# Second spectral product of a convolution and Fourier-mixing kernel: the 64-channel part as two products at TensorE row places 0 and 64, one PSUM tile and one store per half

## Chip, cores, metric

The kernel runs on one core of a Trainium2 chip. A time is the device time of one execution in microseconds (us), from the device's own counter. The profile is one execution recorded by the hardware profiler: its span is the time from the first to the last instruction of the program on that core.

## What is computed

The input is 32 images of 56 x 56 places with 96 channels, in float32. Each image goes through two layers. The first is a layer norm, a product to 192 channels, a 3 x 3 convolution back to 96, SiLU, and the residual. The second takes the 3136 places as a sequence and runs a Fourier mixing step and a feed-forward step. The change lies in the Fourier mixing step, which in the reference reads:

```python
h = jnp.einsum('bnc,hc->bnh', x, w1)
h = jax.nn.relu(_bn(h, bn1_gamma, bn1_beta, bn1_mean, bn1_var))
X = jnp.fft.fft(h, axis=1, norm='ortho')
xr = jax.nn.relu(X.real * rd - X.imag * idg + rb)
xi = jax.nn.relu(X.imag * rd + X.real * idg + ib)
y = jnp.fft.ifft(xr + 1j * xi, axis=1, norm='ortho').real.astype(jnp.float32)
o = jnp.einsum('bnh,ch->bnc', y, w2)
return _bn(o, bn2_gamma, bn2_beta, bn2_mean, bn2_var)
```

There are 192 channels before the product with w2 and 96 after it. Because w2 acts on channels alone, the kernel applies it to the spectrum, ahead of the inverse transform.

## The kernel before

**Stages.** Each image passes through the steps of the class `Image`: layer norm and image layout (`im`), convolution in three groups of 32 output channels (`cv`, lines 182 and 186), back to places (`st`, line 219), second norm and turn to channels (`tp_n`, line 158), product with w1 (`ph`, line 232), the first half of the transform (`pa`, line 241), a trip through DRAM that regroups the places (`da`, `at`), the second half of the transform (`px`, line 256), scale and ReLU of the spectrum into `gt`, the product with w2 (`pg`, lines 295 and 299), the first half of the inverse (`pe`, line 309), a second trip through DRAM (`de`, written at line 501, read into `y` at line 507), the last part of the inverse (`py`, line 317), and the feed-forward step in fp8 (`tp_n` line 156, `pf` line 328, `po` line 342). Work of several images is in flight at a time.

**The stage that is changed.** The 28 pages of an image's spectrum are worked in four units of 8, 8, 8 and 4 pages (`UNITS`). A page is a matrix of 192 channels by 112 columns (114 in the first unit). Channels 0 to 127 of a page fill the 128 partitions of `gt[:, 0]` or `gt[:, 1]`. The last 64 channels of two pages share the partitions of `gt[:, 2]`: channels of a page of the unit's first half lie at partitions 0 to 63, those of the matching page of its second half at partitions 64 to 127. So one `gt[:, 2, j]` belongs to two pages.

`product_w2` (line 289) takes two such pairs at a time, chosen by `four` (line 284). For each pair it issues one product over 128 partitions with the weights `w2y`, which are 192 columns wide and zero in the off-diagonal blocks, so that one result holds both pages side by side (line 295). Then it adds, for each of the two pages, a product over 128 partitions with `w2x`, 96 columns wide (line 299). Both pairs lie in one PSUM tile `pg`. ScalarE copies it to `gw` (line 301), `inverse` multiplies each page by its table (line 309) into `pe`, ScalarE copies that to `es` (line 311), and `store_back` (line 496) issues two stores to `de`. Each image has 14 pairs: 14 products at line 295 and 28 at line 299.

**Records.** TensorE's stationary operand here is the page (112 or 114 columns) and the moving operand the weights. Each float32 matmul of these lines is two records of the trace (a weight load and a product each), so that 448 products of line 295 appear as 896. The text calls such a record a pass.

**What sets the order.** The kernel keeps a list `order` of steps with due times; `plan` (line 570) puts them there in units of an eighth of an image. `second_w2`, `second_back` and `store_back` of a unit are due at fixed distances (lines 653 to 657). The list's order is the priority with which the framework's scheduler lays out each engine's instructions when the kernel is built; a step whose inputs or buffers it expects late falls behind others. On the chip each engine then runs its list in that order. `pg`, `pe`, `pa` and `po` share the two PSUM buffers of the tag `b`.

**Tiles of the array.** The convolution puts four products of 32 columns side by side at column places 0, 32, 64 and 96 of the array, and `px` of the last 64 channels puts two of 64 columns at column places 0 and 64 (line 256, the form 112*64 in the trace; 112*128 is the whole array). All other products of a steady image address the array as a whole.

Of the kernel before, what the change touches and what calls it, by code (L numbers as in the profile page):

```python
# [38 lines left out]
F32 = mybir.dt.float32  # L39
# [6 lines left out]
C = 96  # L46
# [5 lines left out]
PG = 4  # L52
NS = NP // PG
UNITS = ((0, 8), (8, 16), (16, 24), (24, 28))
# [20 lines left out]
def width(p):  # L75

    return 2 * N2 + (p < UNITS[0][1])
# [8 lines left out]
def hybrid_kernel(ctx: ExitStack, tc: tile.TileContext, x, par, spar, cpar, w_in, conv_w, w1, w2, fw1, fb1, fw2, fb2, fa, fb, ib, ia, rows6, out):  # L86
    nc = tc.nc
    nb = x.shape[0]

    const = ctx.enter_context(tc.tile_pool(name="const", bufs=1))  # L90
# [12 lines left out]
    ib_sb = const.tile([114, NP, 112], F32, name="ib_sb")  # L103
# [6 lines left out]
    rows6_sb = const.tile([N1, 2 * WC * WG], F32, name="rows6_sb")  # L110
    w1a = const.tile([C + 1, H], F32, name="w1a")
    w2x = const.tile([128, C], F32, name="w2x")
    w2y = const.tile([128, 2, C], F32, name="w2y")
    w1q = const.tile([C, FF], F8, name="w1q")
    w2q = const.tile([128, 3, C], F8, name="w2q")
    b1q = const.tile([128, 3], F32, name="b1q")
# [164 lines left out]
        nc.vector.scalar_tensor_tensor(gt[:, u, :n, 0, :], sv[:, 0], rb, av[:, 1], ALU.add, ALU.max)  # L281
        nc.vector.scalar_tensor_tensor(gt[:, u, :n, 1, :], sv[:, 2], 0.0, sv[:, 1], ALU.max, ALU.subtract)  # L282

    def four(m, j0):

        p0, p1 = UNITS[m]
        return [[p0 + half * (p1 - p0) // 2 + j0 + j for j in range(2)] for half in range(2)]

    def product_w2(gt, b, m, j0):
        k = 2 * width(UNITS[m][0])  # L290
        pg = psum2.tile([k, 2, 2, C], F32, tag="b", name=f"pg_{b}_{m}_{j0}")
        for j in range(2):

            lhs = gt[:, 2, j0 + j].rearrange("c r k -> c (r k)")
            nc.tensor.matmul(pg[:, :, j, :], lhs, w2y, start=True, stop=False, skip_group_check=True)  # L295
            for half in range(2):
                p = four(m, j0)[half][j] - UNITS[m][0]
                lhs = gt[:, p // PG, p % PG].rearrange("c r k -> c (r k)")
                nc.tensor.matmul(pg[:, half, j, :], lhs, w2x, start=False, stop=True, skip_group_check=True)  # L299
        gw = work.tile([k, 2, 2, C], F32, tag="gw", name=f"gw_{b}_{m}_{j0}")  # L300
        nc.scalar.copy(gw.rearrange("k h j c -> k (h j c)"), pg.rearrange("k h j c -> k (h j c)"))
        return gw

    def inverse(gw, b, m, j0):

        pe = psum2.tile([112, 2, 2, C], F32, tag="b", name=f"pe_{b}_{m}_{j0}")
        for half, ps in enumerate(four(m, j0)):
            for j, p in enumerate(ps):
                nc.tensor.matmul(pe[:, half, j, :], ib_sb[: gw.shape[0], p, :], gw[:, half, j, :], start=True, stop=True)  # L309
        es = work.tile([112, 2, 2, C], F32, tag="es", name=f"es_{b}_{m}_{j0}")  # L310
        nc.scalar.copy(es.rearrange("k h j c -> k (h j c)"), pe.rearrange("k h j c -> k (h j c)"))
        return es

    def transform_out(y, b, g):
# [170 lines left out]
            im.gt[m] = work.tile([128, 3, PG, 2, w], F32, tag="gt", name=f"gt_{im.b}_{m}")  # L485
        relus(*im.held.pop(("sv", m, u)), im.gt[m], u)

    def second_w2(im, m, j0):
        im.gw[m, j0] = product_w2(im.gt[m], im.b, m, j0)

    def second_back(im, m, j0):
        if m + j0 == 0:
            im.de = dram.tile([NP, 112, C], F32, tag="de", name=f"de_{im.b}")
        im.held["es", m, j0] = inverse(im.gw.pop((m, j0)), im.b, m, j0)

    def store_back(im, m, j0):
        p0, p1 = UNITS[m]
        es = im.held.pop(("es", m, j0))
        rows = im.de[p0:p1].rearrange("(h j) m c -> m h j c", h=2)
        for half in range(2):  # L500
            nc.sync.dma_start(rows[:, half, j0 : j0 + 2], es[:, half])

    def fetch_y(im, g):
        if g < NG:
# [65 lines left out]
    def plan(b):  # L570
        im = Image(b)

        def put(when, f, *args):
            order.append((8 * b + when, len(order), lambda: f(im, *args)))

        last = b == nb - 1
        CONV, FIRST, BACK, FFN = ALL
        S0, SS = 0, 2
        if nb - 4 < b < nb - 1:
            BACK, FFN = BACK + 0.4, FFN + 0.284  # L580
        if last:

            CONV, FIRST, FFN = CONV - 0.074, FIRST - 0.016, FFN - 0.721
            S0, SS = -0.831, 2.033
        back_step, ffn_step = (0.82, 0.962) if last else (0.775, 0.971)

        for i, (j0, j1) in enumerate(LN_CHUNKS):
            at = CONV - 2.485 + 0.531 * i
            ahead = 12 if b == 0 else 2.489 - 0.157 * i
            put(CONV - 7.98 + 0.01 * i if b == 1 else at - ahead, fetch, i)  # L590
            put(at - 0.551, take_in, i)
            for j in range(0, j1 - j0, 2):
                put(at + 0.08 * j, make_image, i, j)
            put(CONV + (5.967 if b else 5.7) + 1.132 * i, norm_b, i)
            put(FIRST + 2 * i - (0.477 if b else 0.6), deviation, i)
            if b:
                put(CONV - 0.346 + 0.78 * i, load, i)
        put(CONV - 0.078, make_seam)
        for r in range(NR if b else 0):
            at = CONV + 1.91 * r  # L600
            for part, when in enumerate((0, 0.139, 1.039)):
                put(at + when, conv_part, r, part)
            put(at + 0.72, conv_first, r)
            put(at + 1.252, conv_last, r)
            for half in range(2):
                put(at + 1.757 + 0.21 * half, conv_tokens, r, half)
                put(at + 1.858 + 0.21 * half, conv_end, r, half)
        if b == 0:

            at = CONV  # L610
            for r in range(NR + 1):
                steps = []
                if r < NR:
                    steps += [(conv_part, r, 0), (conv_part, r, 1), (conv_part, r, 2), (conv_first, r)]
                if r:
                    steps += [(conv_tokens, r - 1, 0), (conv_end, r - 1, 0)]
                    steps += [(conv_tokens, r - 1, 1), (conv_end, r - 1, 1)]
                if r < NR:
                    steps += [(conv_last, r)]
                for f, *args in steps:  # L620
                    put(at, f, *args)
                    at += 0.214
        for g in range(NG):
            at = FIRST + g
            put(at - 0.407, tokens_a, g)
            for j2 in range(2):
                put(at + 0.065 + 0.371 * j2, forth, g, j2)
                put(at + 0.536 + 0.659 * j2, forth_a, g, j2)
            put(at + 1.2, store_a, g)
# [12 lines left out]
            put(at + 0.986, ffn_end, g)  # L642
            put(at + 1.497, store, g)
        for g in range(NS):
            put(max(FIRST + 7.433, S0 + g - (1.479 if g % 2 else 1.674)), fetch_a, g)
        for m, (p0, p1) in enumerate(UNITS):
            both = p1 - p0 > PG
            for at, u in ((0, 0), (0.606, 1), (1.099, 2)) if both else ((0.088, 0), (0.674, 2)):
                at += S0 + SS * m + (0.125 if m + u == 0 else 0)
                put(at, second, m, u)  # L650
                put(at + 0.22, second_parts, m, u)
                put(at + 0.47, second_relus, m, u)
            for j0 in range(0, (p1 - p0) // 2, 2):
                at = S0 + SS * m + (2.024 if both else 1.221) + 0.062 * j0
                put(at, second_w2, m, j0)
                put(at + 0.2, second_back, m, j0)
                put(at + 0.575, store_back, m, j0)

    def load(im, i):
        im.load(i)  # L660
# [3 lines left out]
    for b in range(nb):  # L664
        plan(b)
# [15 lines left out]
    with tc.tile_pool(name="setup", bufs=1) as sp, tc.tile_pool(  # L681
        name="setup_ps", bufs=2, space=bass.MemoryType.PSUM
# [16 lines left out]
        for g in range(2):  # L699
            ps = spp.tile([128, 512], F32, tag="ps", name=f"ps_wt{g}")  # L700
# [6 lines left out]
        for y in range(3):  # L707
            ps = spp.tile([128, 512], F32, tag="ps", name=f"ps_we{y}")
# [89 lines left out]
    def make_w2():  # L798
# [2 lines left out]
        scale, bias = bn_fold("2", BN2, 1)  # L801
        tc.keep_in_program_order(nc.vector.tensor_scalar(w2s[:, :H], w2s[:, :H], scale, None, ALU.mult))
        tc.keep_in_program_order(nc.vector.tensor_copy(w2s[:, H:], w2s[:, 128:H]))
        nc.gpsimd.memset(w2y, 0.0)
        ps = bank("w2")
        for g in range(2):
            nc.tensor.transpose(ps[:, g * C : (g + 1) * C], w2s[:, g * 128 : (g + 1) * 128], ident[:C, :C])
        tc.keep_in_program_order(nc.vector.tensor_copy(w2x, ps[:, :C]))
        for i in range(2):
            tc.keep_in_program_order(nc.vector.tensor_copy(w2y[64 * i : 64 * i + 64, i, :], ps[64 * i : 64 * i + 64, C : 2 * C]))  # L810
# [156 lines left out]
```

## Time and profile before

| quantity | value |
|---|---|
| median of three runs | 3042.79 us (3034.49 to 3044.51) |
| span of the profiled execution | 3036.8 us |
| TensorE (PE) busy | 2978.4 us, 98% |
| VectorE (DVE) busy | 2348.2 us, 77% |
| ScalarE (ACT) busy | 2277.4 us, 75% |
| line 295 (`pg` with `w2y`) | 896 passes, mean 335 ns |
| line 299 (`pg` with `w2x`) | 1792 passes, mean 258 ns |
| stores `de` (line 501) | 448, 84.0 KB each, 2.0 us to landing |

The page of the profile does not list a whole time of the profiled execution beside its span; the median of the runs is 6.0 us above the span (3042.79 - 3036.8), which is taken as what lies around it. A busy time of PE counts a product from its start to its modelled end, and successive products overlap, so mean durations cannot be added up. What a stretch costs is read from the timeline instead, as the distance between the start of its first row and the start of the row that follows it. The granted clock is 1.00 between 300 and 2800 us, so that durations of that stretch can be compared directly.

### The profile page before, as it was taken

How to read it: one execution, taken by the hardware profiler on the slowest of the kernel's cores; microseconds unless marked ns; L12 is line 12 of the kernel's file. 1: busy time of each engine (PE TensorE's matmuls, PEld its weight loads, DVE VectorE, ACT ScalarE, POOL GpSimd, SP SyncE). 2: the span in 40 equal slices, each digit the busy share in tenths (PEclk: the TensorE clock that was granted, in tenths of full speed). 3: DMA queues.
4: the chain of work that ended last, by engine and by line, in shares of the span. 5: the costliest groups of instructions: out<-in, count | busy, mean ns of one | idle time of the engine just before them, and what ended most of it. 6: DMA issues, size and time to landing. Idle time of an engine off the chain costs nothing.

```text
span 3036.8 us, 84414 instructions
## 1 busy us (share of the span) xinstructions
PE 2978.4 (98%) x32693; PEld 2445.3 (81%) x32693; DVE 2348.2 (77%) x7248; ACT 2277.4 (75%) x5703; POOL 647.5 (21%) x398
## 2 busy tenths in 40 slices
PE   8999999999999999999999999999999999999997
PEld 7678788888888887888888888888888888888775
DVE  5548777888778887778887778887778887777778
ACT  3467777787777787777787777787777877777877
POOL 2202122222112221122221222221222221121111
PEclk9899999999999999999999999999999999999998
DMA  3533444443454444444444444434444434444443
GB/s 85 144 93 94 117 126 124 118 123 98 121 133 126 117 116 108 122 130 122 123 109 114 125 126 123 127 98 122 124 128 122 123 96 124 129 129 104 113 123 78
DMA packets 495435, 355.37 MB, mean 117 GB/s; under 512 B 329992, under 2 KB 459304, under 8 KB 494808
## 3 DMA queue, kind: packets, MB, share of 16 engines
q1 hardware_dynamic: 493146, 349.24, 43.5%
q8 instruction: 257, 4.21, 0.6%
q10 hardware_dynamic: 1888, 0.74, 0.1%
q14 instruction: 144, 1.18, 0.1%
HBM read 195.73 MB, written 154.14 MB: 115 GB/s over the span
## 4 chain that ended last, share of the span: by engine, by line
PE 88%; DMA 5%; DVE 3%; ACT 2%; issue 1%; POOL 0%; SPq 0%; ACTq 0%; DVEq 0%
PE cv L186 14%; PE ph L232 10%; PE px L256 10%; PE pa L241 9%; PE im L165 7%; PE pe L309 6%; PE pg L299 5%; PE py L317 5%; PE pg L295 5%; PE po L342 4%; PE pf L328 4%; PE cv L182 3%; PE st L219 3%; PE tp_n L158 2%; DMA de<-es 2%; DMA xl<-in_x 1%
## 5 line engine op out<-in xcount | busy, mean ns | idle before, releaser
L186 PE MATMUL cv<-img,wv 97*32 97x196 f32 x13248 | 621.6, 331 | 0.0
L147 POOL TENSOR_TENSOR rs_c<-var_c,mhalf 112x8 f32<-112x8 f32 (+1 forms) x128 | 206.7, 1615 | 1894.1 <-DVE var_c L145 879.1
L186 PEld LDWEIGHTS cv<-img,wv 97*32 97x32 f32 x13248 | 426.8, 109 | 106.9
L235 ACT ACTIVATE h<-ph,rs_b 112x192 f32<-112x192 f32 x896 | 340.1, 449 | 74.1 <-PE ph L232 74.0
L232 PE MATMUL ph<-w1a,n2t 97*112 97x192 f32 x1792 | 381.2, 335 | 2.0 <-ACT n2t L225 0.9
L241 PE MATMUL pa<-h,fa_sb 112*112 112x384 f32 x896 | 372.3, 497 | 0.8 <-ACT h L235 0.8
L330 ACT CAST h<-pf 128x448 f16<-128x448 f32 x672 | 367.5, 567 | 1.1 <-PE pf L328 1.0
L256 PEld LDWEIGHTS px<-fb_sb,at 112*64 112x64 f32 (+1 forms) x3584 | 319.2, 166 | 58.1 <-issue 8.7
L256 PE MATMUL px<-fb_sb,at 112*64 112x112 f32 (+3 forms) x3584 | 353.5, 272 | 8.1 <-DMA at<-da 4.0
L165 PE MATMUL im<-rows_sb,xa 112*97 112x168 f32 x1792 | 321.2, 313 | 2.1 <-DVE xa L410 1.4
L232 PEld LDWEIGHTS ph<-w1a,n2t 97*112 97x112 f32 x1792 | 278.5, 177 | 47.4 <-issue 18.1
L147 POOL TENSOR_TENSOR rs_b<-var_b,mhalf 112x8 f32<-112x8 f32 (+1 forms) x128 | 227.7, 1788 | 397.3 <-DVE var_a L145 310.2
L165 PEld LDWEIGHTS im<-rows_sb,xa 112*97 112x97 f32 x1792 | 264.1, 168 | 33.1 <-issue 15.7
L242 ACT COPY u<-pa 112x384 f32<-112x384 f32 x448 | 226.2, 505 | 75.6 <-PE pa L241 75.4
L272 DVE SCALAR_TENSOR_TENSOR sv<-px,spar_sb,av 128x224 f32<-128x224 f32 (+2 forms) x352 | 152.9, 434 | 151.3 <-ACT av L263 149.8
L336 DVE CAST hq<-h 128x448 fp8e5<-128x448 f16 x672 | 256.1, 386 | 7.5
L335 DVE TENSOR_SCALAR h<-h,b1q 128x448 f16<-128x448 f16 x672 | 220.1, 329 | 40.6 <-ACT h L330 36.1
L299 PE MATMUL pg<-w2x,gt 128*112 128x96 f32 (+1 forms) x1792 | 243.1, 258 | 0.0
L167 ACT COPY img<-im 97x336 f32<-97x336 f32 x448 | 205.5, 461 | 48.6 <-PE im L165 25.8
L299 PEld LDWEIGHTS pg<-w2x,gt 128*112 128x112 f32 (+1 forms) x1792 | 240.8, 178 | 0.0
L261 ACT ACTIVATE av<-px,spar_sb 128x224 f32<-128x224 f32 (+2 forms) x352 | 162.8, 462 | 100.9 <-PE px L256 99.1
L295 PE MATMUL pg<-w2y,gt 128*112 128x192 f32 (+1 forms) x896 | 226.8, 335 | 1.1 <-DVE gt L282 0.7
(121 smaller groups left out, 6197.6 us busy)
## 6 DMA issues: line engine op xcount, KB each, us to landing
da<-u SPq DMA_DIRECT2D x224, 336.0 KB, 3.1
at<-da SPq DMA_DIRECT2D x224, 336.0 KB, 4.2
de<-es SPq DMA_DIRECT2D x448, 84.0 KB, 2.0
y<-de SPq DMA_DIRECT2D x224, 168.0 KB, 2.5
out<-t SPq DMA_DIRECT2D x224, 168.0 KB, 2.6
t<-in_x SPq DMA_DIRECT2D x96, 336.0 KB, 4.4
xl<-in_x SPq DMA_DIRECT2D x93, 336.0 KB, 4.5
t<-in_x SPq DMA_DIRECT2D x32, 168.0 KB, 3.8
```

The costliest lines, as they stand in the source:

```text
L147: nc.gpsimd.tensor_tensor(rs, var, mhalf[:, :n], ALU.pow)
L165: nc.tensor.matmul(ps[:, j], xa[:, j, :], rows6_sb, start=True, stop=True)
L186: tc.keep_in_program_order(nc.tensor.matmul(*args, start=(dx == 0), stop=(dx == 2)))
L232: nc.tensor.matmul(ph[:, j, :], n2t[:, 2 * j2 + j, :], w1a, start=True, stop=True)
L235: nc.scalar.activation(h[:, j], ph[:, j], AF.Relu, scale=rs[:, 2 * j2 + j : 2 * j2 + j + 1])
L241: nc.tensor.matmul(pa, fa_sb, h, start=True, stop=True)
L242: nc.scalar.copy(u[:, 2 * j2 : 2 * j2 + 2, :], pa)
L256: nc.tensor.matmul(px[rows, j], lhs, fb_sb[:, first(p) : first(p + 1)], start=True, stop=True)
L295: nc.tensor.matmul(pg[:, :, j, :], lhs, w2y, start=True, stop=False, skip_group_check=True)
L299: nc.tensor.matmul(pg[:, half, j, :], lhs, w2x, start=False, stop=True, skip_group_check=True)
L330: nc.scalar.copy(h1, pf)
L336: nc.vector.tensor_copy(hq[:, k, :], h2, saturate=False)
```

## The change

`w2y` loses its zero blocks: it is 96 columns wide, with the same 64 rows of weights once at partitions 0 to 63 and once at 64 to 127. A unit's product is made in two calls, one per half of its pages. The first call allocates a PSUM tile for each half and issues, for every pair, two products over 64 partitions each: partitions 0 to 63 (row place 0) into the tile of half 0, partitions 64 to 127 (row place 64) into the tile of half 1. These 8 products (4 in the last unit) stand together; all but the first are marked to be placed with high priority, in program order. The products with `w2x` of half 0 follow, then in the second call those of half 1. Copies, inverse and store go by halves: one copy to `gw`, one PSUM tile `pe`, one copy to `es` and one store for each. The due times of the two calls lie 0.124 apart, as those of the two blocks of a unit of 8 pages did.

```diff
-    w2y = const.tile([128, 2, C], F32, name="w2y")
+    w2y = const.tile([128, C], F32, name="w2y")
...
-        for j in range(2):
-
-            lhs = gt[:, 2, j0 + j].rearrange("c r k -> c (r k)")
-            nc.tensor.matmul(pg[:, :, j, :], lhs, w2y, start=True, stop=False, skip_group_check=True)
-            for half in range(2):
-                p = four(m, j0)[half][j] - UNITS[m][0]
-                lhs = gt[:, p // PG, p % PG].rearrange("c r k -> c (r k)")
-                nc.tensor.matmul(pg[:, half, j, :], lhs, w2x, start=False, stop=True, skip_group_check=True)
...
+    def product_w2(pg, gt, b, m, half):
+
+        k, n = 2 * width(UNITS[m][0]), pages(m)
+        products = []
+        if half == 0:
+            pg += [psum2.tile([k, n, C], F32, tag="b", name=f"pg_{b}_{m}_{i}") for i in range(2)]
+            for j in range(n):
+                for i in range(2):
+                    rows = slice(64 * i, 64 * i + 64)
+                    lhs = gt[rows, 2, j].rearrange("c r k -> c (r k)")
+                    products.append((pg[i][:, j], lhs, w2y[rows], j == 0, False))
+        for j in range(n):
+            p = half * n + j
+            lhs = gt[:, p // PG, p % PG].rearrange("c r k -> c (r k)")
+            products.append((pg[half][:, j], lhs, w2x, False, j == n - 1))
+        for at, (to, lhs, rhs, start, stop) in enumerate(products):
+            args = dict(start=start, stop=stop, skip_group_check=True)
+            if half or at in (0, 2 * n):
+                nc.tensor.matmul(to, lhs, rhs, **args)
+                continue
+            with tc.high_priority():
+                tc.keep_in_program_order(nc.tensor.matmul(to, lhs, rhs, **args))
+        gw = work.tile([k, n, C], F32, tag="gw", name=f"gw_{b}_{m}_{half}")
+        nc.scalar.copy(gw, pg[half])
         return gw
...
+    def store_back(im, m, half):
+        p0 = UNITS[m][0] + half * pages(m)
+        rows = im.de[p0 : p0 + pages(m)].rearrange("j m c -> m j c")
+        nc.sync.dma_start(rows, im.held.pop(("es", m, half)))
...
-            for j0 in range(0, (p1 - p0) // 2, 2):
-                at = S0 + SS * m + (2.024 if both else 1.221) + 0.062 * j0
-                put(at, second_w2, m, j0)
-                put(at + 0.2, second_back, m, j0)
-                put(at + 0.575, store_back, m, j0)
+            for half in range(2):
+                at = S0 + SS * m + (2.024 if both else 1.221) + 0.124 * half
+                put(at, second_w2, m, half)
+                put(at + 0.2, second_back, m, half)
+                put(at + 0.575, store_back, m, half)
```

In the setup the zeroing of `w2y` is dropped and its two copies write 96 columns each. `inverse` has the same products as before, sorted by halves.

More of the change, by code (lines that the diff above doesn't have):

```diff
@@ L282, in relus @@
         nc.vector.scalar_tensor_tensor(gt[:, u, :n, 1, :], sv[:, 2], 0.0, sv[:, 1], ALU.max, ALU.subtract)
[L284 to L291, printed above, removed]
-        for j in range(2):
-            lhs = gt[:, 2, j0 + j].rearrange("c r k -> c (r k)")
-            nc.tensor.matmul(pg[:, :, j, :], lhs, w2y, start=True, stop=False, skip_group_check=True)
-            for half in range(2):
-                p = four(m, j0)[half][j] - UNITS[m][0]
-                lhs = gt[:, p // PG, p % PG].rearrange("c r k -> c (r k)")
-                nc.tensor.matmul(pg[:, half, j, :], lhs, w2x, start=False, stop=True, skip_group_check=True)
-        gw = work.tile([k, 2, 2, C], F32, tag="gw", name=f"gw_{b}_{m}_{j0}")
-        nc.scalar.copy(gw.rearrange("k h j c -> k (h j c)"), pg.rearrange("k h j c -> k (h j c)"))
-        return gw
@@ L304, in inverse, with pages @@
[L304 to L311, printed above, removed]
+    def pages(m):
+        return (UNITS[m][1] - UNITS[m][0]) // 2
@@ L312, in inverse @@
+    def inverse(gw, b, m, half):
+        n = pages(m)
+        pe = psum2.tile([112, n, C], F32, tag="b", name=f"pe_{b}_{m}_{half}")
+        for j in range(n):
+            at = ib_sb[: gw.shape[0], UNITS[m][0] + half * n + j, :]
+            nc.tensor.matmul(pe[:, j, :], at, gw[:, j, :], start=True, stop=True)
+        es = work.tile([112, n, C], F32, tag="es", name=f"es_{b}_{m}_{half}")
+        nc.scalar.copy(es, pe)
         return es
@@ L486, in second_relus, with second_w2, second_back @@
         relus(*im.held.pop(("sv", m, u)), im.gt[m], u)
[L488 to L492, printed above, removed]
-            im.de = dram.tile([NP, 112, C], F32, tag="de", name=f"de_{im.b}")
[L494 to L501, printed above, removed]
+    def second_w2(im, m, half):
+        if half == 0:
+            im.held["pg", m] = []
+        im.gw[m, half] = product_w2(im.held["pg", m], im.gt[m], im.b, m, half)
+    def second_back(im, m, half):
+        if m + half == 0:
+            im.de = dram.tile([NP, 112, C], F32, tag="de", name=f"de_{im.b}")
+        im.held["es", m, half] = inverse(im.gw.pop((m, half)), im.b, m, half)
+    def store_back(im, m, half):
+        p0 = UNITS[m][0] + half * pages(m)
+        rows = im.de[p0 : p0 + pages(m)].rearrange("j m c -> m j c")
+        nc.sync.dma_start(rows, im.held.pop(("es", m, half)))
     def fetch_y(im, g):
@@ L803, in make_w2 @@
         tc.keep_in_program_order(nc.vector.tensor_copy(w2s[:, H:], w2s[:, 128:H]))
-        nc.gpsimd.memset(w2y, 0.0)
         ps = bank("w2")
@@ L809, in make_w2 @@
         for i in range(2):
-            tc.keep_in_program_order(nc.vector.tensor_copy(w2y[64 * i : 64 * i + 64, i, :], ps[64 * i : 64 * i + 64, C : 2 * C]))
+            tc.keep_in_program_order(nc.vector.tensor_copy(w2y[64 * i : 64 * i + 64, :], ps[64 * i : 64 * i + 64, C : 2 * C]))
         ps = bank("o2")
```

## Prediction

> **What bounds the kernel now.** I read the engine rows of the page first, then the same busy times for the steady stretch, then the timeline of TensorE at three places, then the groups by shape.
>
> ```profile
> PE 2978.4 (98%) x32693; PEld 2445.3 (81%) x32693; DVE 2348.2 (77%) x7248; ACT 2277.4 (75%) x5703; POOL 647.5 (21%) x398
> ...
> PE py L317 <- DMA y<-de: 10.1, 11, 3.4
> ...
> 300.00:2800.00 2500.00, 2492.87 (x27790) 2056.53 (x27789) 1979.06 (x6099) 1924.37 (x4831) 552.78 (x325) 1.00 0.45 120
> ```
>
> The first line is the page's, the second is PE's longest wait in total, the third the steady window (PE, weight loads, DVE, ACT, POOL busy; clock; DMA share). PE idles 7.1 of 2500 us there, at the full clock, while DVE (1979) and ACT (1924) have over 500 us free. So PE's own list of work is the time, and an edit counts by the PE time that it adds or removes. All waits for the second DRAM trip are 10.1 us.
>
> The second look is one unit of the changed stage, all 8 pages in a row:
>
> ```profile
> 1484.90 0.54 PE L295 MATMUL pg<-w2y,gt 128*112 128x192 f32 x2
> 1485.28 0.54 PE L299 MATMUL pg<-w2x,gt 128*112 128x96 f32 x4
> 1485.65 0.50 PE L295 MATMUL pg<-w2y,gt 128*112 128x192 f32 x2
> 1485.99 0.54 PE L299 MATMUL pg<-w2x,gt 128*112 128x96 f32 x4
> 1486.37 0.50 PE L295 MATMUL pg<-w2y,gt 128*112 128x192 f32 x2
> 1486.71 0.54 PE L299 MATMUL pg<-w2x,gt 128*112 128x96 f32 x4
> 1487.09 0.51 PE L295 MATMUL pg<-w2y,gt 128*112 128x192 f32 x2
> 1487.43 0.54 PE L299 MATMUL pg<-w2x,gt 128*112 128x96 f32 x4
> 1487.81 0.35 PE L328 MATMUL pf<-n3t,w1q 96*128 96x448 fp8e5 x1
> ```
>
> From start to start, the four wide products take 0.38 + 0.34 + 0.34 + 0.34 = 1.40 us and the eight narrow ones 0.37 + 0.38 + 0.38 + 0.38 = 1.51 us. A pass of 192 columns thus costs 0.175 us, one of 96 columns 0.094 us. The narrow pass is no cheaper although its moving side is halved, since each also loads a page of 112 columns: the eight passes of `pe`, again 112 loaded and 96 moving, run from 1399.88 to the next row at 1400.65, 0.096 us each. I take 0.096 us as the floor that a 112-column load sets.
>
> The third look is what TensorE does when it changes between the whole array and column places:
>
> ```profile
> 1405.38 0.81 PE L232 MATMUL ph<-w1a,n2t 97*112 97x192 f32 x4
> 1406.03 0.35 PE L328 MATMUL pf<-n3t,w1q 96*128 96x448 fp8e5 x1
> ...
> 1522.85 0.90 PE L232 MATMUL ph<-w1a,n2t 97*112 97x192 f32 x4
> 1523.69 1.00 PE L256 MATMUL px<-fb_sb,at 112*64 112x114 f32 x16
> 1524.62 0.35 PE L182 MATMUL cv<-img,wv 97*32 97x196 f32 x1
> ...
> 1526.75 0.91 PE L232 MATMUL ph<-w1a,n2t 97*112 97x192 f32 x4
> 1527.50 0.81 PE L241 MATMUL pa<-h,fa_sb 112*112 112x384 f32 x2
> ```
>
> The same four passes of `ph` take 0.65 us between whole-array neighbours, 0.75 us right after a convolution (1526.75 to 1527.50), and 0.84 us after one and ahead of the `px` that uses column places (1522.85 to 1523.69). So being first after a change costs 0.10 us (nothing of the weights was loaded ahead) and being last before one costs 0.09 us (the next load starts only when the product is out). A visit to another arrangement and back has two of each: 0.38 us.
>
> ```profile
> L256 PE MATMUL px<-fb_sb,at 112*128 112x112 f32 x1280 | 169.4, 276 | 1.5 <-DVE t L516 1.5
> L256 PE MATMUL px<-fb_sb,at 112*64 112x112 f32 x1280 | 82.5, 267 | 0.0
> ```
>
> Equal numbers of passes, busy 169.4 us with the whole array and 82.5 us at two column places: there, two products run at once. In the timeline the 16 passes take 0.93 us with 0.09 of change in them, 0.05 each.
>
> **The change part by part.** The order of TensorE's instructions in the built kernel says how the new products stand. In 64 units all 8 stand together; in 31 the first one is placed earlier, alone, and 7 follow; of the short units 28 have 4 together and 4 have 1 and 3; the first image has 8 alone. That is 170 visits to the row places.
>
> Removed: 448 wide products, 1.40 / 4 = 0.35 us each: 156.8 us.
>
> Added: 896 products over 64 partitions, 1792 passes. The trace has no product at row places. Bounds: two at once, each pair of passes at the load floor, 0.096 us, as the column places do; or one after the other, 0.096 us per pass. I take pairs, since the nearest row (112*64) pairs fully. A run of 8, 7, 4, 3 or 1 products takes 8, 8, 4, 4 or 2 such slots: 64 x 8 + 31 x (8 + 2) + 28 x 4 + 4 x (4 + 2) + 8 x 2 = 974 slots, 93.5 us. One after the other: 1792 x 0.096 = 172.0 us.
>
> Added: 170 visits. Bounds: nothing, if a change of row place is none for the array, and 0.38 us each, 64.6 us. I take 0.38, the price of every change of arrangement that the trace shows.
>
> The narrow products stay 1792 passes, now without a wide one before them that loads ahead: 1792 x 0.096 = 172.0 us against 448 x 1.51 / 4 = 169.1 us, +2.9 us.
>
> Moved with them: the built order changes between whole array and places 1077 times against 668 before; 340 are the 170 visits, which leaves 69 more by `cv` and `px`. One such visit is 0.09 and 0.10 on the way out and 0.09 and about a quarter of 0.10 on the way in for 32 columns, 0.31 us: 69 / 2 x 0.31 = 10.7 us.
>
> Hidden: ACT gets 64 more copies (the short unit's, halved), 0 to 0.48 us each (the median of `gw`); I take 0, as ACT has 23% free, and without that cover it would be up to 31 us. SP issues 192 fewer stores at 0.45 us, 86 us off its queue; behind them stand the fetches of `y`. The last store of an image is now due 0.124 of an eighth of 91.7 us later, 1.4 us, but between the last `pe` and the first `py` the built order has 9.6 or 11.2 us of PE work by turns where it had 9.9. PE's wait for `y` was 10.1 us in all: at best -10, at worst 0.3 us x 32 = +10; I take 0. Setup loses one memset, nothing.
>
> The wait that is added: both PSUM buffers of tag `b` must be free for the row-place products, since these write both halves. Queued behind a waiting product are all of PE's next items, and `pa`, `po` and `pe` use the same buffers. Bounds: 0, or one ACT copy of 0.48 us for each of 128 units, 61 us. PE's waits for `gw` were 0.7 us in all, so I take 0.
>
> Sum: -156.8 + 93.5 + 64.6 + 2.9 + 10.7 = +14.9 us, made against the span of 3036.8 us; the runs' median lies 6.0 us above it, and carries over: 3042.8 + 14.9 = 3058 us.
>
> **Two rules from the skill.** The Trainium skill, TensorEngine Tiling (Array Packing), Key Properties, says that going to another tiling mode, not merely another tile, drains TensorE; it gives no time, and the 0.09 us above agrees, for column places. The Trainium skill, TensorE: Matmul & The Clock Gate, Measured speedup vs the span model, reports 3.07 times for four row tiles; an estimate from that, 1.53 for two, would make 1792 / 1.53 = 1171 slots, 112.4 us, and the sum +33.8 us, 3077 us. No run here shows it yet.
>
> **Rivals.** *Free row places* (the other side): the array need not empty between whole rows and row places, because the columns stay 112 wide. Then the 64.6 us go: -49.7 us, 2993 us. It wins from a visit under 0.38 - 14.9 / 170 = 0.29 us. For it: all changes seen are of columns. Against: each of them costs the same 0.09 us, whatever the widths.
>
> *No pairs*: the loads of two row places follow each other, and the load sets the pace. +78.5 us more, 3136 us. For it: 112 columns of weights are as many as the whole array loads, where the paired rows load 64. Against: in the 112*64 row neither loads nor products follow one another.
>
> *Buffer waits*: half of the 61 us, 3088 us. For it: the first product stands alone in 35 units, so the scheduler expected the second buffer late there. Against: the 0.7 us.
>
> **How the numbers follow.** Forecast 0.50 (3058, its own range 3040 to 3080); free row places 0.22 (2993); no pairs 0.15 (3136); buffer waits 0.13 (3088). The range 2990 to 3110 leaves out no pairs and little else. A measurement can tell 0.3%, 9.1 us: faster is below 3033.7, slower above 3051.9. Faster: 0.22 and 0.02 of the forecast's spread. Same: 0.15 of the forecast. Slower: the remaining 0.33 of it, 0.15 and 0.13.
>
> **What would show it.** Right: products over 64 rows start in pairs some 10 ns apart, pairs 0.096 us apart; the pass before and the first after them are longer by 0.09 and 0.10 us; PE stays above 99% busy in the steady stretch. Wrong: passes of 64 rows 0.09 us apart one by one (no pairs); no longer neighbours (free row places); idle PE ahead of the new lines put down to ACT `gw`, `u`, `y` or `es` (buffer waits). The forecast falls if several small terms, each from two or three rows, lean one way, as +14.9 is small beside 156.8.

## The result, and the profile after

The changed kernel takes 3068.17 us (median of 4 runs, 3067.48 to 3071.0) against 3042.36 us before (4 runs, 3034.49 to 3044.51): a ratio of 1.0086, 95% interval 1.0071 to 1.0101, so 25.8 us slower. Its profiled run took 3067.48 us with a span of 3065.7 us, 28.9 us over the span before. The 1.8 us between its time and its span is what lies around a span; the runs of the kernel before that were measured later show the same 1.8. The 6.0 us given ahead of the prediction are thus 4 us too many: the profiled execution before was about that much faster than the median, which is why the spans differ by more than the medians.

The engine row of its page, and its steady stretch (PE, weight loads, DVE, ACT, POOL busy; granted clock; DMA share; GB/s):

```profile
PE 3004.8 (98%) x33589; PEld 2397.3 (78%) x33589; DVE 2345.1 (76%) x7248; ACT 2281.7 (74%) x5767; POOL 632.7 (21%) x397
```

```profile
300.00:2800.00 2500.00, 2492.48 (x28250) 1992.69 (x28249) 1961.82 (x6059) 1912.33 (x4850) 535.14 (x324) 1.00 0.46 118
```

PE is as busy as before (2492.48 of 2500 us, before 2492.87), at the same clock. So by the page the loss is longer PE work and not longer gaps (short waits that it doesn't show come below): PE's busy time rose by 26.4 us. PE's wait for the second DRAM trip (total us, times, longest):

```profile
PE py L327 <- DMA y<-de: 7.7, 10, 2.5
```

The wait for `y` fell from 10.1 to 7.7 us; the only longer one in total, of `st` for ScalarE, is 7.9 us where it was 7.2. Waits for ScalarE's copy `gw` are still 0.7 us. Next the timeline of PE at a unit whose row-place products stand together:

```profile
1492.39 0.81 PE L232 MATMUL ph<-w1a,n2t 97*112 97x192 f32 x4
1493.13 0.33 PE L305 MATMUL pg<-w2y,gt 64*112 64x96 f32 x1
1493.14 0.33 PE L308 MATMUL pg<-w2y,gt 64*112 64x96 f32 x1
1493.30 0.26 PE L305 MATMUL pg<-w2y,gt 64*112 64x96 f32 x1
1493.31 0.85 PE L308 MATMUL pg<-w2y,gt 64*112 64x96 f32 x13
1494.09 0.43 PE L305 MATMUL pg<-w2x,gt 128*112 128x96 f32 x2
1494.36 0.75 PE L308 MATMUL pg<-w2x,gt 128*112 128x96 f32 x6
1494.95 0.95 PE L305 MATMUL pg<-w2x,gt 128*112 128x96 f32 x8
1495.74 0.74 PE L165 MATMUL im<-rows_sb,xa 112*97 112x168 f32 x4
```

A unit's first product stands at L305, the ones marked with high priority at L308. So the first two rows of `w2y` are its first products at row place 0 and at row place 64: they start 0.01 us apart, a pair runs at once. The 16 row-place passes take 1493.13 to 1494.09, 0.96 us; the 16 narrow ones 1.65 us; and the `ph` ahead lasts 0.74 us instead of 0.65: in the trace the first weight load of the row places starts only at 1493.13, with their first product, so nothing is loaded ahead across the change of form (from whole array to row or column places, or back). Together 0.96 + 1.65 + 0.09 = 2.70 us, where the unit took 1.40 + 1.51 = 2.91 us before: 0.21 us gained. And a unit whose first product was placed earlier:

```profile
1471.67 0.81 PE L241 MATMUL pa<-h,fa_sb 112*112 112x384 f32 x2
1472.41 0.43 PE L305 MATMUL pg<-w2y,gt 64*112 64x96 f32 x2
1472.77 1.15 PE L256 MATMUL px<-fb_sb,at 112*128 112x112 f32 x8
1473.75 0.35 PE L338 MATMUL pf<-n3t,w1q 96*128 96x448 fp8e5 x1
1473.94 0.81 PE L232 MATMUL ph<-w1a,n2t 97*112 97x192 f32 x4
1474.60 0.35 PE L338 MATMUL pf<-n3t,w1q 96*128 96x448 fp8e5 x1
1474.88 1.02 PE L308 MATMUL pg<-w2y,gt 64*112 64x96 f32 x14
1475.83 0.43 PE L305 MATMUL pg<-w2x,gt 128*112 128x96 f32 x2
1476.10 0.75 PE L308 MATMUL pg<-w2x,gt 128*112 128x96 f32 x6
1476.69 0.95 PE L305 MATMUL pg<-w2x,gt 128*112 128x96 f32 x8
1477.48 0.35 PE L338 MATMUL pf<-n3t,w1q 96*128 96x448 fp8e5 x1
1477.67 1.04 PE L256 MATMUL px<-fb_sb,at 112*128 112x112 f32 x8
```

Two passes at place 0 alone take 0.36 us, the other 14 take 0.95, the narrow ones 1.65. To these come the neighbours: `pa` 0.74 instead of 0.65 us, the first `px` group 0.98 where the second one takes 0.88, `pf` 0.28 where another takes 0.19. In sum 3.24 us, 0.33 more than before. So whole runs gain and split ones lose more: a split adds one visit and two slots that nothing shares.

**Prices.** From start to start over 300 to 2700 us, the pass before a change of form costs 92 ns extra (`ph` ahead of the row places 255 ns, ahead of `pf` 162 ns) and the first pass after it 75 ns (the first narrow pass after a row-place run 174 ns, the others 99 ns). A change is 0.167 us, a visit 0.334 us. The first number holds for every form (91 to 94 ns ahead of row places and of both kinds of column places); the second depends on the pass that comes first (75 ns for `pg` and `pe`, 88 to 92 for `px`, `ph` and `pa`), so 0.167 us for changes other than those of the row places is an approximation. A pair of row-place passes takes 0.099 us, as a narrow pass does. By these prices a short unit with its 4 products in one piece takes 4 x 0.099 + 0.334 + 8 x 0.099 = 1.52 us, against 2 x 0.35 + 1.51 / 2 = 1.46 before: it loses, though nothing splits it.

### The profile page after: what moved, and what is told of

It reads as the page before. It is cut to its first block, busy times and chain, and to the rows that moved or that the text cites. A ratio compares the mean times of both kernels' runs of the same rounds, so it can differ in the third digit from the quotient of the medians.

```text
span 3065.7 us, 86119 instructions
## 1 busy us (share of the span) xinstructions
PE 3004.8 (98%) x33589; PEld 2397.3 (78%) x33589; DVE 2345.1 (76%) x7248; ACT 2281.7 (74%) x5767; POOL 632.7 (21%) x397
## 4 chain that ended last, share of the span: by engine, by line
PE 73%; DVE 12%; ACT 6%; DMA 6%; issue 2%; POOL 1%; SPq 0%; POOLq 0%; ACTq 0%; DVEq 0%
PE cv L186 13%; PE ph L232 8%; PE px L256 8%; PE pa L241 7%; PE im L165 6%; PE pg L305 5%; PE py L327 4%; PE pe L319 4%; PE pg L308 4%; PE cv L182 3%; PE po L352 3%; PE pf L338 3%; PE st L219 2%; PE tp_n L158 2%; DMA de<-es 2%
## 5 line engine op out<-in xcount | busy, mean ns | idle before, releaser
L186 PE MATMUL cv<-img,wv 97*32 97x196 f32 x13248 | 633.0, 331 | 0.0
L340 ACT CAST h<-pf 128x448 f16<-128x448 f32 x672 | 358.0, 556 | 28.4 <-PE pf L338 28.1
L256 PE MATMUL px<-fb_sb,at 112*64 112x112 f32 (+3 forms) x3584 | 360.2, 273 | 7.6 <-DMA at<-da 4.2
L241 PE MATMUL pa<-h,fa_sb 112*112 112x384 f32 x896 | 364.0, 493 | 1.0 <-ACT h L235 1.0
L338 PE MATMUL pf<-n3t,w1q 96*128 96x448 fp8e5 x672 | 223.0, 357 | 4.0 <-ACT h L340 2.6
L319 PEld LDWEIGHTS pe<-gw,ib_sb 112*112 112x112 f32 (+1 forms) x1792 | 202.5, 178 | 24.9 <-issue 5.3
L147 POOL TENSOR_TENSOR rs_a<-var_a,mhalf 112x8 f32<-112x8 f32 (+1 forms) x128 | 210.5, 1660 | 51.2 <-DVE var_a L145 51.2
```

Source lines behind the costliest of these rows:

```text
L147: nc.gpsimd.tensor_tensor(rs, var, mhalf[:, :n], ALU.pow)
L186: tc.keep_in_program_order(nc.tensor.matmul(*args, start=(dx == 0), stop=(dx == 2)))
L241: nc.tensor.matmul(pa, fa_sb, h, start=True, stop=True)
L256: nc.tensor.matmul(px[rows, j], lhs, fb_sb[:, first(p) : first(p + 1)], start=True, stop=True)
L319: nc.tensor.matmul(pe[:, j, :], at, gw[:, j, :], start=True, stop=True)
L338: nc.tensor.matmul(pf, w1q[:, k * 128 : (k + 1) * 128], n3t, start=True, stop=True)
```

## Experiments

A run gives its median, and its ratio to the kernel before measured beside it. All twelve kernels do the whole work of the reference. Due times are in eighths of an image, so that 0.1 is 1.1 us (0.1 x 91.8 / 8); the expectations of runs 9, 10 and 12 call them us.

**1. The halved structure without row places.** The weights `w2y` get their zero blocks back, and every row-place product becomes one over all 128 partitions, in the place where it stands.

```diff
-                    rows = slice(64 * i, 64 * i + 64)
-                    lhs = gt[rows, 2, j].rearrange("c r k -> c (r k)")
-                    products.append((pg[i][:, j], lhs, w2y[rows], j == 0, False))
+                    lhs = gt[:, 2, j].rearrange("c r k -> c (r k)")
+                    products.append((pg[i][:, j], lhs, w2y[:, i], j == 0, False))
```

> The changed kernel's halves, PSUM tiles, order and stores, but without row places: each 64-channel product runs over all 128 partitions with zeros in the other page's rows. Theory (a loaded page of 112 columns sets 0.096 us per pass, a visit to places costs 0.38 us): 1792 passes at 0.096 us are 172.0 us where the wide products took 156.8 (+15.2), the other narrow passes +2.9, no visits to row places, and the built order has 751 changes between whole array and column places where it had 668 (83 / 2 x 0.31 = +12.9): 3042 + 31 = 3073 us. So row places as placed in the changed kernel would be worth only about 5 us (3073 - 3068). Rival (the loss of the changed kernel is in the visits and the rest of the change costs nothing): 3060 us or less.

Measured: 3092.72 us, ratio 1.0177 (1.0155 to 1.0198). That is 20 us above the expectation, which gave the row places only 5 us. So the halves with 96-column products cost 53 us by themselves, the changes and waits of their order included, and the row places win some 25 us of it back, visits included (24.5 us between the two medians, 27.6 between the two losses). That they do nothing but harm is wrong; they can't pay for the narrow products.

**2. Runs in one piece.** For half 0 the narrow products go first and the row-place products follow as one run; the last of them ends half 0.

```diff
-                for i in range(2):
+                for i in (1, 0):
...
+        if half == 0:
+            products = products[2 * n :] + products[: 2 * n]
+            products = [(to, lhs, rhs, at == 0 or (at == n), at >= n) for at, (to, lhs, rhs, _, _) in enumerate(products)]
...
-            if half or at in (0, 2 * n):
+            if half or at in (0, n):
```

> The products over 128 partitions of half 0 come first, then all row-place products, the first of them into the second half's tile, so that they start only when both PSUM buffers are there and no unit's run is split (128 visits instead of 170, 896 slots instead of 974). Theory (the loss is in the visits and the split runs): 896 x 0.096 + 128 x 0.38 + 2.9 + (723 - 668) / 2 x 0.31 - 156.8 = -10.8, 3031 us; down to 3010 if all images take the 90.7 us that those without split runs take in the changed kernel. Rival (the halves themselves cost: two PSUM buffers held at once, later stores): no gain over the changed kernel, 3060 us or more, with PE idle ahead of the new lines.

Measured: 3218.9 us, ratio 1.0588 (1.0566 to 1.0609). The expectation missed by 188 us. The products themselves did what they should (start to start the row-place passes take 110.5 us, 125.8 in the changed kernel), but PE now waits. By tile:

```profile
PE py L330 <- DMA y<-de: 78.2, 28, 5.0
PE py L330 <- ACT h L235: 18.6, 26, 0.7
```

One of these waits in PE's timeline, and the windows around it (length; PE, weight loads, DVE, ACT, POOL busy; granted clock; DMA share; GB/s):

```profile
1491.03 1.62 PE L330 MATMUL py<-y,ia_sb 113*112 113x384 f32 x2 [4.42 <-DMA y<-de]
```

```profile
1488.00:1491.00 3.00, 0.00 (x0) 0.00 (x0) 0.21 (x1) 0.00 (x0) 0.00 (x0) 0.71 0.45 133
1491.00:1494.00 3.00, 2.97 (x10) 2.34 (x10) 1.31 (x4) 0.00 (x0) 0.00 (x0) 0.50 0.61 176
1494.00:1498.00 4.00, 4.00 (x50) 2.19 (x49) 1.66 (x5) 1.71 (x4) 0.00 (x0) 0.50 0.08 28
1498.00:1502.00 4.00, 4.00 (x21) 3.38 (x14) 1.65 (x4) 1.47 (x4) 0.00 (x0) 0.50 0.01 4
```

PE stands for 4.42 us, and then has the granted clock 0.50 for at least 11 us, though it is busy for nearly all of them. Half of 11 us is lost again, so the idle time is charged about twice. The clock records of the trace show it for the whole run: between 300 and 2800 us PE waits 22 times for 2.1 to 4.4 us, 64 us in sum; after 20 of these waits the clock is at 0.50 for 3.4 to 13.7 us, 174 us in sum. PE is busy for 166 of them, so that 83 us are lost again.

The wait has two sides. Between the last `pe` of an image and its first `py` stand 9.3 us of PE work in the trace, where the kernel before has 10.3 (images 7 to 26, the wait itself left out). And the data come later: from that last `pe` to the image's last store of `de` pass 4.0 us, from the store to the fetch of `y` 5.7 us, before 3.5 and 4.4. In the instance shown, SP starts the store at 1481.79 us, it lands at 1488.46, and SP issues the fetch at 1488.51, when PE has been waiting for almost two. So of the rival, later stores have a part in it; PE does not idle ahead of the new lines.

**3. Runs in one piece, the pairs apart.** As 2, with all products at row place 64 ahead of those at 0.

```diff
-            for j in range(n):
-                for i in (1, 0):
+            for i in (1, 0):
+                for j in range(n):
```

> As together, but all row-place products of half 1 stand before all of half 0, so that neighbours share a row place. Theory (two row places run at once only where neighbours alternate): the 896 slots become nearly 1792, +86 us on together at most, 3100 to 3117 us. Rival (each row place works off its own list, whatever the order): as together, 3031 us.

Measured: 3197.61 us, ratio 1.0515 (1.0484 to 1.0546). In time this says little, as its waits differ from those of run 2. By start to start, the row-place passes take 155.8 us, 45.3 more than in run 2, so running in pairs is worth at least that much. A run of 16 passes in its timeline:

```profile
1433.50 0.43 PE L308 MATMUL pg<-w2y,gt 64*112 64x96 f32 x2
1433.78 1.22 PE L311 MATMUL pg<-w2y,gt 64*112 64x96 f32 x14
1434.93 0.34 PE L308 MATMUL pg<-w2x,gt 128*112 128x96 f32 x1
```

1.43 us, where the same run in pairs takes 0.96 and 16 passes one by one would take 16 x 0.099 + 0.167 = 1.75. So the second place still overlaps the first in part: in the trace it starts 0.47 us after it, when four passes have run alone.

**4. Runs in two pieces.** As 2, with half of the narrow products, half of the run, then the rest: one more visit for each of 128 units, and no slot that a pair doesn't share.

```diff
+            narrow, paired, h = products[:n], products[n:], n // 2
+            products = narrow[:h] + paired[: 2 * h] + narrow[h:] + paired[2 * h :]
```

> As together, but each unit's run of row-place products is cut in two with whole-array products between: the same 896 slots, 256 visits instead of 128, and 671 instead of 723 changes by column places. Theory (a visit costs 0.38 us): together + 48.6 - 8.1, 3072 us. Rival (row places cost little to enter, and the loss of the changed kernel came with the split runs' buffers): within 10 us of together.

Measured: 3067.03 us, ratio 1.0084 (1.0066 to 1.0103), near the 3072 that were expected, and 152 us under run 2, although it does more. Its wait of `py` for `y` is 9.7 us. The built order has changed with the edit, and the starving is gone.

**5. Runs in one piece with a later back stage,** meant to give `y` more cover: in 2, `BACK` is 8.086 instead of 8.036.

> As together, with the due time of the inverse's last part (py, BACK) 0.05 of an eighth of an image later, nothing else. In the built order PE then has about 2 us more work between an image's last pe and its first py. Theory (together lost its time to PE standing idle for y, 78 us in all, and to the clock that the idle stretches cost; its row places cost what the trace of the changed kernel shows): the wait shrinks to the 10 us of the kernel before, and 896 x 0.096 + 128 x 0.38 + 2.9 + (701 - 668) / 2 x 0.31 - 156.8 = -14 us against the kernel before, 3025 us; up to 3036 if the 11 us by which the changed kernel exceeded its forecast come again. Rival (together's stall comes from holding both PSUM buffers or from the stores by halves): the wait for y or for ScalarE stays, 3100 us or more.

Measured: 3100.04 us, ratio 1.0184 (1.0169 to 1.0200). A miss again. The wait for `y` shrank to 14.3 us, but others came:

```profile
PE ph L232 <- ACT h L235: 25.7, 27, 1.0
PE py L330 <- DMA y<-de: 14.3, 13, 5.0
```

**6 and 7. The two edits of 3 and 4 on top of 5.**

> As late, but all row-place products of half 1 stand before all of half 0. Theory (products run at once only where the other row place comes up within a few instructions; together_apart shows four passes alone, some pairs, four alone): together_apart spent 155.8 us from start to start on its row-place products where together spent 110.5, so late + 45 us. Rival (order within the run does not matter): within 8 us of late.

> As late, but each unit's run of row-place products is cut in two: 256 visits instead of 128, the same 896 slots, 700 changes by column places instead of 701. Theory (0.38 us a visit): late + 49 us. Rival (the visit is cheaper than the rows of the kernel before suggested, for instance only the 0.09 us at the ends): late + 23 us or less.

Measured: 3130.23 us, ratio 1.0291 (1.0272 to 1.0310), and 3125.5 us, ratio 1.0276 (1.0251 to 1.0300): 30 and 25.5 us above run 5, where 45 and 49 were expected. Start to start the changed lines grew as expected: `pg` at the row places by 45.3 us in run 6, both `pg` lines by 47.3 us for 128 visits in run 7 (0.37 us each over the whole run; 0.34 in steady images). In its time alone run 7 lies nearer to the rival of a cheaper visit (23 us or less); the start-to-start times decide against it. Most of the rest was given back by shorter waits elsewhere: by the measure of short waits explained below, they are about 0.4 us per steady image fewer in both runs than in run 5, some 12 us.

**8. Runs in one piece with the unit's end due earlier:** in 2, eight-page units are due at 1.924 instead of 2.024.

> As together, with the product by halves of the 8-page units due 0.1 earlier instead of py later. Theory: the wait for y is covered this way too (11.2 to 11.6 us of PE work between last pe and first py where together had 9.8), and the changes by column places are 690: 86.0 + 48.6 + 2.9 + 3.4 - 156.8 = -16 us, 3023 us, or up to 11 us more. Rival (only py's own due time matters): a wait for y as in together, 3100 us or more.

Measured: 3159.55 us, ratio 1.0378 (1.0362 to 1.0394). The wait for `y` is back to 9.8 us, and a new one stands in the list:

```profile
PE po L355 <- DVE hq L349: 49.1, 17, 5.5
```

**9 to 11. Three more orders of the same runs,** each with one due time moved in 2.

```diff
-    CONV, FIRST, BACK, FFN = -15.042, -8.232, 8.036, 10.805
+    CONV, FIRST, BACK, FFN = -15.042, -8.232, 8.036, 10.705
```

> Row-place runs in one piece (all 14 paired products of a unit one after the other, before or behind the narrow ones), and the feed-forward work planned 0.1 us earlier than in the run together, which orders the other work differently: 671 changes of array form outside the row-place runs where the run together has more, and about 12.0 us of PE work between the last pe product of an image and its first py product (the run together 9.8, the kernel before 10.8). Theory A, that PE's own ledger sets the time: wide products away -153.7 us, row-place slots +87.8, slower narrow w2x products +7.8, visits of the row places and other changes of form +46.6: in sum about -11.5 against the kernel before, so about 3030 us. Theory B, that a re-ordered schedule opens waits of PE for y, h, es or hq, as it did in together, late and early: 3060 to 3160. What tells them apart: the waits of PE by tile; under A no line of them is over 10 us besides those of the kernel before.

Measured: 3050.5 us (10 runs, 3041.51 to 3060.74), ratio 1.0046 (1.0030 to 1.0061). The best of the runs in one piece, under the band of theory B and yet 20 us above theory A. Waits for `y` are up:

```profile
PE py L330 <- DMA y<-de: 18.9, 15, 5.1
```

With the eight-page units due at 1.85 instead:

> Row-place runs in one piece, with the second half of the eight-page units due 0.17 us earlier than in the run together: 691 changes of array form outside the row-place runs, about 10.7 us of PE work between the last pe product and the first py product, as the kernel before has (10.8). Theory A, that PE's own ledger sets the time: about -8 against the kernel before, so about 3034 us. Theory B, that the re-ordered schedule opens waits of PE: 3060 to 3160. The waits of PE by tile tell them apart, the wait of py for y above all, which should be under 15 us if the 10.7 us are enough cover.

Measured: 3074.11 us, ratio 1.0117 (1.0096 to 1.0138). Theory A falls here too. Both halves of these units come earlier by the edit. `y` is well covered: 10.0 us of PE work stand ahead of it, and from the last `pe` to the last store and on to the fetch pass only 2.7 and 4.7 us. The loss is in many short waits, of some kinds about one an image:

```profile
PE py L330 <- DMA y<-de: 12.6, 13, 2.3
...
PE im L165 <- DVE xa L423: 6.6, 27, 0.3
...
PE tp_n L156 <- ACT h L343: 6.3, 30, 0.9
```

With `FIRST` at -8.132 instead:

> Row-place runs in one piece, with the first stage planned later than in the run together: 697 changes of array form outside the row-place runs, about 11.6 us of PE work between the last pe product and the first py product. Theory A, that PE's own ledger sets the time: about -7 against the kernel before, so about 3035 us. Theory B, that the re-ordered schedule opens waits of PE: 3060 to 3160. If the three kernels of this kind all come out over 3060 with waits on different tiles, the gain of the row places in one piece is eaten by whichever supply the new order starves, and not by one tile.

Measured: 3229.17 us, ratio 1.0629 (1.0602 to 1.0656). The worst of all, with waits on three other tiles and a mean granted clock of 0.962 over the span, where the kernel before has 0.990:

```profile
PE po L355 <- DVE hq L349: 64.5, 30, 3.4
PE pe L322 <- ACT u L242: 22.1, 28, 0.9
PE pf L341 <- ACT h L343: 17.6, 32, 1.2
```

**12. The changed kernel with more of its runs split,** by `BACK` 8.086 alone.

> The changed kernel with its back stage planned 0.05 us later, and nothing else: in the built order the row-place runs of 127 units are split by other products (the changed kernel splits far fewer), which makes 1154 slots of row-place passes and 532 changes into and out of them. Theory A, that what the changed kernel loses is set by how often the runs are split: -153.7 + 1154 x 0.098 (113.1) + 7.8 + 566 more changes at 0.18 (102) = +69 against the kernel before, so about 3110 us. Rival: the split runs cost nothing that counts and the time stays by the changed kernel's, about 3068 us.

Measured: 3154.27 us, ratio 1.0385 (1.0365 to 1.0406). The rival, that splits don't count, is out; the 118 us are also more than the 69 expected. The row-place passes rose to 159.7 us from start to start (changed kernel 125.8), as 1154 slots of 0.099 us and 266 visits at half of 0.334 us ask (158.7), but a wait came with the order:

```profile
PE ph L232 <- ACT h L235: 26.9, 28, 1.0
```

It accounts for 27 of the missing 49 us. By the measure of short waits in the next section this run has 1.5 us an image more of them than the kernel before, 1.1 of it ahead of `ph`: 48 us in 32 images.

## Why the prediction was right

The side was right and the size right to 11 us: +14.9 forecast, +25.8 measured (+28.9 by the spans). The steps, per steady image (images 7 to 26 of both traces, first `py` to first `py`; the forecast's terms divided by 32):

| term | forecast, us | measured, us | how measured |
|---|---|---|---|
| wide products gone | -4.90 | -4.79 | start to start |
| row-place slots | +2.92 | +2.97 | 30 x 0.099 |
| visits | +2.02 | +1.67 | 5 x 0.334 |
| slower `w2x` products | +0.09 | +0.23 | 56 x 0.0988 against 5.30 |
| other changes of form | +0.33 | +0.42 | 2.5 x 0.167 |
| waits | 0 | +0.44 | below |
| sum | +0.47 | +0.94 | all of PE: +1.00 |

Without the waits the sum is +0.50, next to the forecast's +0.47. That closeness is partly luck: the visits came out 0.35 us cheaper and the four other terms together 0.39 dearer.

*Visits* were the right mechanism at a price 0.046 us too high. This also settles the rival of free row places: row places empty the array as column places do, at 92 ns. The Trainium skill (TensorEngine Tiling (Array Packing), Key Properties) has the rule without a time, and these rows agree with it.

*Pairs* were right, which puts out the rival without pairs: starts 0.01 us apart, and 45.3 us lost when the order of run 3 takes half of the sharing away. The estimate of 1.53 times that the prediction worked out from the Trainium skill (TensorE: Matmul & The Clock Gate, Measured speedup vs the span model) was too low here: a whole run puts 16 passes into 8 slots of the same 0.099 us, 2.0 times. *Buffer waits* don't show: 0.7 us of waits for `gw`, and from start to start no pass ahead of a row-place run is more than 2 ns above the usual price of the change (103 runs between 300 and 2700 us whose last two passes ahead are of one tile).

*The load floor* of 0.096 us was an average with the cheap first pass in it. In a row of equal passes every one takes 0.099 us; after a wide product the first narrow one took 82 ns, and the changed kernel has no wide ones. Hence slots and `w2x` are both dearer.

*Waits at nothing* is the step that failed in size. The row of PE's waits showed no more of them, and yet PE's distances from the last pass of one tile to the first of another, where the form stays, are in sum 0.90 us an image over their usual values (the 20th percentile of that kind of pass, the two products of `pg` left out), before 0.46. Nearly all of the difference stands ahead of `im` (0.26), `tp_n` (0.13), `pf`, `st` and `po` (0.07 to 0.08 each), while those ahead of `ph` fell by 0.11. Each such wait is a few tenths of a us (`pf` to `im` takes 0.45 to 0.71 us in three places between 1000 and 1400 us, else 0.19), which falls under the modelled end of the product before, so the page counts most of it as busy. The waits of the weight loads show some of them:

```profile
PEld im L165 <- ACT img L167: 9.9, 21, 1.0
```

Before, the weight loads of `im` waited 3.6 us in 11 times for this copy. They come from the built order, which shifted with the change. The same two terms, PE's ledger and the short waits, explain the other orders that don't starve for long (us per steady image against before; for runs 9 and 10, eight images without a long wait that I chose, against all images of the kernel before):

| kernel | changes of form | ledger | short waits | sum | measured |
|---|---|---|---|---|---|
| changed kernel | 33.5 | +0.50 | +0.44 | +0.94 | +1.00 |
| 1, whole array | 23.5 | +1.38 | +0.22 | +1.60 | +1.55 |
| 4, split in two | 37 | +0.88 | -0.03 | +0.85 | +0.92 |
| 9, feed-forward earlier | 29 | -0.45 | +0.33 | -0.12 | -0.10 |
| 10, units due earlier | 30 | -0.29 | +0.94 | +0.65 | +0.71 |
| 5, later back stage | 30 | -0.29 | +1.85 | +1.56 | +1.99 |
| 12, more splits | 38 | +1.84 | +1.5 | +3.3 | +3.56 |

The kernel before has 21 changes. A ledger is PE's own work at these prices: -4.79, the row-place slots at 0.099 (28 in one piece, 30 in the changed kernel, 36 in run 12), +0.23, and 0.167 for each change above 21; for run 1 it is +0.73 (56 passes of 99 ns for 28 wide ones), +0.23 and the changes. Run 5, with most waiting, fits worst. Over all of images 7 to 26, as in the other rows, run 9 comes to +0.46 and run 10 to +0.99, so the -0.10 of run 9 is no gain over the kernel before. The short waits and the measured time come from the same trace, so this shows where the time is, and not why the order makes those waits.

So the expected gain of pairing is real, about 1.8 us an image (2.97 against 4.79), and goes into 12.5 more changes of form (2.1 us), the dearer narrow passes (0.2) and short waits (0.4). Runs in one piece would gain 0.45 us an image at most, 14 us or 0.5%, and no order I tried had both that and few waits: run 9 is 0.46% above the kernel before, and none of the twelve is below it. Whether an order exists that keeps the 14 us stays open. Which supply each order starves was read from the waits; why the built order leaves `hq` or `h` late in runs 5, 8, 11 and 12 I did not trace.

The images of the changed kernel last 90.7 and 94.6 us by turns. That is no cost of its own: by turns they hold 384 and 480 of the convolution's passes, where every image before holds 432, and run 1, without row places, alternates too (91.0 and 95.4).

## What to carry to other kernels

When products are moved to parts of the array, count the changes of form in the order as built and price each (0.167 us here) before counting what the sharing saves: half-height pairs gained only where a visit held eight products in one piece. In a kernel whose first engine is 99.7% busy, treat every edit as a re-ordering of the whole list: here six orders of the same products, whose changes of form differ by 9 us in all (927 to 979), took from 3050 to 3229 us. Look for waits in each, the short ones by start-to-start distances. In run 2, PE's waits of 2.1 to 4.4 us cost more than their length once more in the clock (64 us of waiting, 83 us at half speed).

## What the runs showed of the hardware that was not expected

After PE stood for 4.42 us, its granted clock was 0.50 for at least 11 us, although PE was busy again (run 2). The Trainium skill (TensorE: Matmul & The Clock Gate, What's actually happening) names an idle window of about 3.4 us for the fall, and at least one such window of sustained work for the return. The low stretches of run 2 between 300 and 2800 us last 3.4, 6.8, 10.2 or 13.7 us, which fits windows of that length. Two things go beyond it: the stretch shown ended only after 11.9 us of work, and the clock also fell after waits of 2.2 to 2.5 us, counted from the modelled end of the product before (after 2.19 us at 1388.3, for example).

The order of the pairs matters: with the eight passes of one row place ahead of the eight of the other, the second place started 0.47 us after the first, when four passes had run alone (run 3). Its first pass then started at 1433.98 us, ahead of the last three of the first place (1434.07 to 1434.27), which stand before it in the program. And the loads of the two row places, like the products, don't wait for one another: in the unit shown of the changed kernel the first two start 7 ns apart, and each pair takes 0.099 us, what a single narrow pass with its load takes. That the load sets this pace is seen in the widths: with 114 columns loaded instead of 112, and the same 96 moving, a narrow pass takes 0.100 instead of 0.098 us.
